# Layer 0 of a four-layer cross-attention stack by heads: raw exponentials transposed, their sums from matmuls of ones, the division after the value product, and a schedule one tick shorter

## The chip, the cores and the metric

The kernel runs on one core of a Trainium2 chip. The metric is device time in microseconds. Three timed runs of the kernel before gave 2430.0, 2432.49 and 2432.74, median 2432.49. The execution that the hardware profiler recorded took 2433.93, of which 2431.9 is the span of the trace.

## The reference, cut to what matters

All is in float32. There are B = 8 sequences of S = 256 tokens of width D = 128, and for each a context of M = 64 vectors of width 64. Layer 0, the part that changes, is attention of the tokens to the context with 16 heads of 8 channels:

```python
q = (x @ Wq.T).reshape(B, L, H, D).transpose(0, 2, 1, 3)      # H=16 heads of 8
k = (ctx @ Wk.T).reshape(...) + pos ;  v = (ctx @ Wv.T).reshape(...)
attn = softmax(q @ k.T * 8 ** -0.5)                            # over 64 context vectors
memory_output = (attn @ v).reshape(B, L, D) @ Wo.T
gate = sigmoid(silu([x, mean(ctx)] @ gate_w1.T + gate_b1) @ gate_w2.T + gate_b2)
enhanced = layernorm(x + gate * memory_output)
x = where(entropy(softmax(x @ ent_w.T)) > 1, enhanced, x)      # per sequence
```

Layer 1 is one more cross attention with one head, layer 2 is six blocks of self attention over 256 tokens with 16 heads of 64, cross attention to the context with 16 heads, and a feed-forward part; layer 3 is a last attention with a layer norm.

## The kernel before

A sequence is two tiles of 128 tokens. The tiles of layer 0 are worked through one by one, n = 2b + qt, n = 0 to 15, and all work of the kernel is laid out by hand on a grid of ticks: `at(tick, phase, step)` puts a step at a place, and at the end all steps are issued by tick, then by phase, with an ordering edge between each instruction and the one before it on its engine. So TensorE (PE), VectorE (DVE), ScalarE (ACT) and GpSimd (POOL) each work in the order of the plan, strictly. DMAs are not held by these edges.

In layer 0 a tile passes four ticks (`plan_weights_64`, L314). In tick n, phase 1, `scores` makes 16 small matmuls (L328) into a PSUM tile of 128 x 1024: 32 tokens by 16 heads by 64 keys in each group of partitions. In phase 2, `lower` copies it to SBUF on ACT (L357), takes the maximum of each head on DVE (L359) and subtracts it on POOL (L360). In phase 8 ACT takes the exponentials (L366). In tick n+1, phase 2.4, `divide` sums each head's 64 exponentials (L370), takes the reciprocal of 16 sums (L371) on DVE and multiplies on POOL (L372). In tick n+2, phase 2.5, `turn` transposes 32 x 32 blocks on DVE (L380). In tick n+3, phase 3.0, `sums` adds eight matmuls (L388) of the weights with VW, in which the value and output weights are already folded together, and `add` (L687) applies the gate and adds the residual. The same function serves the cross attention of layer 2, with a mask, in which nothing changes.

The fold is made once at the start: `spread_outputs` (POOL, L523), `turn_values` (PE L530, ACT L533), `fold_l0` (PE L545, ACT L552); for each sequence `values_of` multiplies it with the context (PE L303) and copies it (ACT L309). In ticks 1 and 2 the start also holds `gate_hidden` (L501 on ACT and L502 on DVE in turns), the mask conversions (DVE L624), `gates` (PE L508) and `logits` (PE L447).

After attention, `moments`, `normal`, `scaled` and `mix` make the layer norm of a sequence, with two transposes on PE in two different ticks (L713, L721) and small operations on POOL (L265 to L696). Layer 1 of the sequence starts two ticks later (`plan_l1`): transposes (L749), weights (L757, L761, L766, L772), another transpose (L780), values (L789, L794). Self attention of sequence b starts with its scores (L898) at tick T0 + 4b, with T0 = 17; its statistics come six ticks ahead, its normalisation (L832) five, its projections (L861, L880) four to one.

All PSUM tiles come from one pool of four slots of two banks each, taken in the order of the plan: the fifth tile waits until the first has been read. The functions that the diff touches follow.

Of the kernel before, what the change touches and what calls it, by code (L numbers as in the profile page):

```python
# [27 lines left out]
def tile_xattn_stack(ctx: ExitStack, tc: tile.TileContext, io, out: bass.AP):  # L28
# [22 lines left out]
    def tp_tile():  # L51
        return one_bank("tp")
# [137 lines left out]
        nc.vector.tensor_copy(hmask8[rows], hmask[rows, 8 * r : 8 * r + 8])  # L190


    W = {}

    def load_sa(l):
# [118 lines left out]
    def plan_weights_64(tick, qt, qT, keys, values, mask, take):  # L314

        tl = {}

        def scores():  # L320
            sc = two_banks("sc").rearrange("p (q x) -> p q x", q=4)
            if mask is None:
                for i in range(4):
                    for a in range(4):
                        q = (i + 2 * (a // 2)) % 4
                        rows = slice(64 * (a // 2), 64 * (a // 2) + 64)
                        qb = 4 * qt + q
                        nc.tensor.matmul(  # L328
                            sc[32 * a : 32 * a + 32, q, :],
                            lhsT=qT()[rows, qb * 32 : (qb + 1) * 32],  # L330
                            rhs=keys()[rows, 4 * (a % 2) : 4 * (a % 2) + 4, :].rearrange(
                                "p h k -> p (h k)"
                            ),
                            start=True, stop=True,
                        )
                tl["sc"] = sc.rearrange("p q x -> p (q x)")
                return
            for q in range(4):
                qb = 4 * qt + q
                for a in range(4):  # L340
                    nc.tensor.matmul(  # L341
                        sc[32 * a : 32 * a + 32, q, :],
                        lhsT=qT()[:, qb * 32 : (qb + 1) * 32],
                        rhs=keys()[:, a].rearrange("p h k -> p (h k)"),
                        start=True, stop=False,
                    )
                for a in range(4):
                    nc.tensor.matmul(
                        sc[32 * a : 32 * a + 32, q, :], lhsT=ones0, rhs=mask,
                        start=False, stop=True,  # L350
                    )
            tl["sc"] = sc.rearrange("p q x -> p (q x)")

        def lower():
            sc = tl.pop("sc")
            e = big("e", shape=(P, 16, M))
            nc.scalar.copy(e.rearrange("p h k -> p (h k)"), sc)  # L357
            m = sm([P, 16], "m16")
            nc.vector.tensor_reduce(m, sc.rearrange("p (h k) -> p h k", k=M), AX.X, ALU.max)  # L359
            nc.gpsimd.tensor_tensor(  # L360
                e, e, m.unsqueeze(2).to_broadcast([P, 16, M]), ALU.subtract
            )
            tl["e"] = e

        def exps():
            nc.scalar.activation(tl["e"], tl["e"], AF.Exp)  # L366

        def divide():
            r = sm([P, 16], "r16")
            nc.vector.tensor_reduce(r, tl["e"], AX.X, ALU.add)  # L370
            nc.vector.reciprocal(r, r)  # L371
            nc.gpsimd.tensor_tensor(  # L372
                tl["e"], tl["e"], r.unsqueeze(2).to_broadcast([P, 16, M]), ALU.mult
            )

        def turn():
            e = tl.pop("e").rearrange("p (q h) (k x) -> p (h k) q x", q=4, x=32)
            eT = big("k" if mask is None else "o", shape=(P, 8, 4, 32))
            for i in range(2):
                nc.vector.transpose(eT[:, 4 * i : 4 * i + 4], e[:, 4 * i : 4 * i + 4])  # L380
            tl["eT"] = eT

        def sums():
            ps = mm_tile()
            eT, vw = tl.pop("eT"), values()
            for s in range(8):
                g, r, k = s // 4, s // 2 % 2, s % 2
                nc.tensor.matmul(  # L388
                    ps[:, :D], lhsT=eT[:, s].rearrange("p q x -> p (q x)"),
                    rhs=vw[:, r, k, g, :], start=(s == 0), stop=(s == 7),  # L390
                )
            take(ps)

        at(tick, 1, scores)
        at(tick, 2, lower)
        at(tick, 8, exps)
        at(tick + 1, 2.4, divide)
        at(tick + 2, 2.5, turn)
        at(tick + 3, 3.0, sums)


    S0 = {}
# [91 lines left out]
            S0["h"].append(ps)  # L494

    def gate_hidden():
        S0["hs"] = [big("k"), big("k")]
        for b in range(B):
            h = S0["hs"][b // 4][:64, (b % 4) * S : (b % 4 + 1) * S]
            ps = S0["h"][b // 4][:64, (b % 4) * S : (b % 4 + 1) * S]  # L500
            nc.scalar.activation(h, ps, AF.Sigmoid, bias=cg[:, b : b + 1])  # L501
            nc.vector.scalar_tensor_tensor(h, ps, cg[:, b : b + 1], h, ALU.add, ALU.mult)  # L502
# [15 lines left out]
        nc.vector.tensor_copy(flag, ps[:, :B])  # L518
        nc.vector.tensor_scalar(nflag, flag, -1.0, 1.0, ALU.mult, ALU.add)

    def spread_outputs():
        S0["wobd"] = place("first", H * D).rearrange("p (h d) -> p h d", h=H)
        nc.gpsimd.tensor_tensor(  # L523
            S0["wobd"], w0o.unsqueeze(1).to_broadcast([P, H, D]),
            hmask.unsqueeze(2).to_broadcast([P, H, D]), ALU.mult,
        )

    def turn_values():
        tps = tp_tile()
        nc.tensor.transpose(tps[:, :DM], w0v, ident[:DM, :DM])  # L530
        wv2 = S0["wv2"] = place("second", P)
        for r in range(2):
            nc.scalar.copy(wv2[:, r * DM : (r + 1) * DM], tps[:, :DM])  # L533

    def fold_l0():


        wobd, wv2 = S0["wobd"], S0["wv2"]
        S0["WVO"] = sb([P, HC, D], "WVO", 1, heap)
        wvo = S0["WVO"].rearrange("p (g a) d -> p a g d", g=2)  # L540
        for half in range(2):
            ps = two_banks("mm")
            for i in range(2):
                a = 2 * half + i
                nc.tensor.matmul(  # L545
                    ps[:, i * 512 : (i + 1) * 512], lhsT=wv2,
                    rhs=wobd[:, 4 * a : 4 * a + 4].rearrange("p h d -> p (h d)"),
                    start=True, stop=True,
                )
            for r in range(2):  # L550
                rows = slice(r * DM, (r + 1) * DM)
                nc.scalar.copy(  # L552
                    wvo[rows, 2 * half : 2 * half + 2],
                    ps[rows].rearrange("p (a g r d) -> p a g r d", a=2, g=2, r=2)[:, :, :, r, :],
                )

    def fold_l1():

# [77 lines left out]
    def plan_start():  # L636
        at(-4, 0, lambda: turn_x(0))
        at(-4, 1, keys_l0)
        at(-4, 2, pool_context)
        at(-1, 0, spread_outputs)  # L640
        for c in range(1, 4):
            at(0, 3.1 + 0.1 * c, lambda c=c: turn_x(c))
        at(0, 3.6, gate_context)
        at(1, 3.0, gate_inputs)
        at(1, 3.1, gate_hidden)
        at(1, 3.2, turn_values)
        for i in range(4):
            at(1, 8.5, lambda i=i: mask(i))
        at(1, 8.6, store_masks)
        at(2, 3.1, fold_l0)  # L650
        at(2, 3.4, gates)
        at(2, 3.6, logits)
        at(3, 4, entropy)
        at(3, 4.1, fold_l1)
        at(4, 4, flags)
        at(4, 4.1, fold_l1_keys)
        at(5, 4, fold_l1_values)
        at(6, 4, fold_l1_outputs)
        at(7, 4, values_l1)
        at(16, 6, mask_keys)  # L660

    def plan_l0(b, T):
        st = {}
# [14 lines left out]
            )  # L678

        def make_values():  # L680
            st["VW"] = values_of(b, S0["WVO"])

        def add(qt, ps):
            if qt == 0:
# [13 lines left out]
        def normal():  # L698
            y = st["y"]
            for j in range(QT):  # L700
                nc.scalar.activation(
                    y[:, j, :], y[:, j, :], AF.Identity, scale=st["rstd"][:, j : j + 1],
                    bias=st["nm"][:, j : j + 1],
                )
            st["kept"] = sb([P, QT, D], "tb", 3)
            nc.scalar.mul(st["kept"], tt(b), nflag[:, b : b + 1])

# [20 lines left out]

        at(T - 2, 3.3, queries)
        at(T - 2, 7, spread_keys)  # L730
        at(T + 2, 3.2, make_values)
        for qt in range(QT):
            plan_weights_64(
                T + qt, qt, lambda: st["q"], lambda: st["k"], lambda: st["VW"], None,
                lambda ps, qt=qt: add(qt, ps),
            )
        at(T + 4, 6, moments)
        at(T + 5, 2.95, normal)
        at(T + 5, 4.8, scaled)
        at(T + 6, 4.7, mix)  # L740

    def plan_l1(b, T):

# [33 lines left out]
        def turn():  # L777
            nc.vector.reciprocal(st["r"], st["r"])
            tps = tp_tile()
            nc.tensor.transpose(tps[:, :P], st.pop("e"), ident)  # L780
            st["eT"] = sb([P, P], "o0")
            nc.scalar.copy(st["eT"], tps[:, :P])

        def values():
# [439 lines left out]
    plan_start()  # L1224
    for b in range(B):
        plan_l0(b, 2 * b)
        plan_l1(b, 2 * b + 7)
    T0 = 2 * B + 1
    T_end = {}
    for l in range(NL):  # L1230
        T_ca = T0 + 4 * B
# [108 lines left out]
```

## Time and profile before

| what | value |
|---|---|
| median of three runs | 2432.49 us |
| the profiled execution | 2433.93 us |
| its span | 2431.9 us, mean granted TensorE clock 0.986 |
| scores of layer 0, first start of ticks 0, 1, 2, 3 | 9.83, 16.60, 22.24, 47.75 us |
| ticks 8 to 13 | 83.43, 89.99, 95.19, 102.62, 107.78, 117.64 us |
| ticks 14, 15 | 129.57, 138.05 us |
| first self-attention scores (tick 17) | 151.90 us |
| L388, one tick | 16 records of 275 ns, about 1.98 us from start to next start |
| L303, one sequence | 32 records, 1.02 us from start to next start |
| L359, L370 | 1222 and 1209 ns |
| L360, L372 | 1902 and 1902 ns |

The page counts each float32 matmul as two records, and the records overlap, so the mean duration of one says less than the distance from one group's start to the next. Start times are from the start of the span. A row of groups gives line, engine, operation, the tiles written and read, shapes and count, then busy us and mean ns, then the idle time of the engine just before and what ended it. The granted clock is TensorE's, 1.00 for full speed.

### The profile page before, as it was taken

How to read it: one execution, taken by the hardware profiler on the slowest of the kernel's cores; microseconds unless marked ns; L12 is line 12 of the kernel's file. 1: busy time of each engine (PE TensorE's matmuls, PEld its weight loads, DVE VectorE, ACT ScalarE, POOL GpSimd, SP SyncE). 2: the span in 40 equal slices, each digit the busy share in tenths (PEclk: the TensorE clock that was granted, in tenths of full speed). 3: DMA queues.
4: the chain of work that ended last, by engine and by line, in shares of the span. 5: the costliest groups of instructions: out<-in, count | busy, mean ns of one | idle time of the engine just before them, and what ended most of it. 6: DMA issues, size and time to landing. Idle time of an engine off the chain costs nothing.

```text
span 2431.9 us, 99981 instructions
## 1 busy us (share of the span) xinstructions
PE 2349.5 (97%) x42411; PEld 1741.0 (72%) x42411; DVE 1836.6 (76%) x5988; ACT 1719.9 (71%) x4528; POOL 1450.3 (60%) x2483
## 2 busy tenths in 40 slices
PE   8999999999999999999999999999999999999997
PEld 4667777677777777777777777777777777777675
DVE  4778887667888667888667888667888667888674
ACT  4567777667777667777667778567778657778662
POOL 3754556755556755556765556765555765555774
PEclk9999999999999999999999999999999999999998
DMA  6000022001022001012000012000013000011000
GB/s 178 2 2 20 20 72 65 2 3 30 20 64 73 3 3 30 20 55 73 12 2 26 23 52 77 12 2 18 25 43 85 21 2 18 25 28 39 2 4 16
DMA packets 102833, 76.87 MB, mean 32 GB/s; under 512 B 8114, under 2 KB 96882, under 8 KB 102387
## 3 DMA queue, kind: packets, MB, share of 16 engines
q1 hardware_dynamic: 101794, 70.16, 10.4%
q8 instruction: 333, 5.46, 1.0%
q14 instruction: 114, 0.93, 0.1%
q10 hardware_dynamic: 592, 0.33, 0.1%
HBM read 62.07 MB, written 8.39 MB: 29 GB/s over the span
## 4 chain that ended last, share of the span: by engine, by line
PE 79%; DVE 7%; ACT 7%; POOL 5%; issue 2%; DMA 0%; SPq 0%; POOLq 0%; DVEq 0%; ACTq 0%
PE mm L861 14%; PE sc L898 14%; PE mm L953 13%; PE mm L971 7%; PE mm L880 7%; PE mm L388 5%; PE sc L341 4%; PE mm L1137 3%; PE mm L1120 3%; DVE m L359 2%; ACT e L357 2%; POOL e L360 2%; PE mm L303 1%; PE tp L841 1%; PE mm L1079 1%
## 5 line engine op out<-in xcount | busy, mean ns | idle before, releaser
L927 POOL TENSOR_SCALAR e<-e,rs 128x256 f32<-128x256 f32 x1536 | 703.1, 478 | 674.9 <-DVE rs L925 665.6
L917 ACT ACTIVATE e<-e,mn 128x256 f32<-128x256 f32 x1536 | 758.2, 495 | 133.7 <-DVE mn L912 129.4
L912 DVE CUSTOM_DVE_ANT_0 e<-sc,nm 128x256 f32<-128x256 f32 x1536 | 542.5, 419 | 108.8 <-PE sc L898 106.2
L937 DVE STREAM_TRANSPOSE eTc<-e 128x512 f32<-128x512 f32 x768 | 517.3, 695 | 62.9 <-POOL e L927 61.6
L898 PE MATMUL sc<-k,q 64*32 64x256 f32 x12288 | 378.3, 380 | 1.9 <-ACT q L867 0.9
L953 PE MATMUL mm<-eTc,v 32*64 32x256 f32 x12288 | 363.7, 378 | 5.7 <-ACT AT L1054 3.3
L953 PEld LDWEIGHTS mm<-eTc,v 32*64 32x64 f32 x12288 | 276.8, 131 | 89.1 <-issue 22.4
L360 POOL TENSOR_TENSOR e<-e,m 128x1024 f32<-128x1024 f32 x112 | 213.1, 1903 | 208.4 <-DVE m L359 208.4
L359 DVE TENSOR_REDUCE m<-sc 128x16 f32<-128x1024 f32 x112 | 136.8, 1221 | 263.8 <-ACT e L357 263.8
L898 PEld LDWEIGHTS sc<-k,q 64*32 64x32 f32 x12288 | 220.9, 106 | 123.3 <-issue 49.6
L917 ACT ACTIVATION_READ_ACCUMULATOR e<-e,mn 128x1 f32 x1536 | 287.2, 187 | 0.0
L341 PE MATMUL sc<-q,tT 128*32 128x256 f32 x3072 | 218.6, 384 | 2.3 <-DVE t L1104 2.3
L372 POOL TENSOR_TENSOR e<-e,r 128x1024 f32<-128x1024 f32 x112 | 213.0, 1902 | 1.2 <-DVE r L371 1.2
L388 PE MATMUL mm<-v,o 128*128 128x128 f32 x1536 | 199.3, 285 | 0.2 <-ACT v L309 0.2
L388 PEld LDWEIGHTS mm<-v,o 128*128 128x128 f32 x1536 | 185.6, 198 | 15.9 <-issue 8.1
L861 PE MATMUL mm<-tT,w_sk 128*128 128x256 f32 x768 | 189.1, 389 | 0.0
L971 PEld LDWEIGHTS mm<-w_sow,o 128*128 128x128 f32 x1536 | 175.1, 192 | 16.2 <-issue 12.3
L880 PE MATMUL mm<-w_sv,tT 128*32 128x256 f32 x3072 | 185.7, 382 | 0.0
L286 ACT COPY v<-mm 128x1024 f32<-128x1024 f32 x96 | 97.2, 1013 | 124.1 <-PE mm L880 123.5
L971 PE MATMUL mm<-w_sow,o 128*128 128x128 f32 x1536 | 183.4, 278 | 0.7 <-ACT WVO L1052 0.7
L861 PE MATMUL mm<-tT,w_sq 128*128 128x256 f32 x768 | 173.6, 379 | 0.0
L861 PEld LDWEIGHTS mm<-tT,w_sk 128*128 128x128 f32 x768 | 138.1, 190 | 44.1 <-issue 29.2
(212 smaller groups left out, 3551.0 us busy)
## 6 DMA issues: line engine op xcount, KB each, us to landing
nm<-mask_d SPq DMA_DIRECT2D x192, 128.0 KB
wd<-o SPq DMA_DIRECT2D x48, 128.0 KB
w_sk<-in_L_sa_kv_dram SPq DMA_DIRECT2D x6, 512.0 KB
w_sv<-in_L_sa_kv_dram SPq DMA_DIRECT2D x24, 128.0 KB
w_sq<-in_L_sa_q_dram SPq DMA_DIRECT2D x6, 512.0 KB
w_sow<-in_L_sa_ow_dram SPq DMA_DIRECT2D x6, 512.0 KB
w_ckv<-in_L_ca_kv_dram SPq DMA_DIRECT2D x12, 256.0 KB
w_cq<-in_L_ca_q_dram SPq DMA_DIRECT2D x6, 512.0 KB
```

Of the source, the lines that this page charges most:

```text
L341: nc.tensor.matmul(sc[32 * a : 32 * a + 32, q, :], lhsT=qT()[:, qb * 32 : (qb + 1) * 32], rhs=keys()[:, a].rearrange("p h k -> p (h k)"), ...
L360: nc.gpsimd.tensor_tensor(e, e, m.unsqueeze(2).to_broadcast([P, 16, M]), ALU.subtract)
L388: nc.tensor.matmul(ps[:, :D], lhsT=eT[:, s].rearrange("p q x -> p (q x)"), rhs=vw[:, r, k, g, :], start=(s == 0), stop=(s == 7),)
L861: nc.tensor.matmul(ps[:, i * S : (i + 1) * S], lhsT=w[:, c * P : (c + 1) * P], rhs=st["tT"], start=True, stop=True,)
L880: nc.tensor.matmul(ps[32 * a : 32 * a + 32, i, :], lhsT=st["tT"][:, kb * 32 : (kb + 1) * 32], rhs=sv[:, a].rearrange("p g x -> p (g x)"), ...
L898: nc.tensor.matmul(sc[32 * a : 32 * a + 32, r, j, :], lhsT=st["q"][g][rows, a, qb * 32 : (qb + 1) * 32], rhs=st["k"][g][rows, a, :], start ...
L912: nc.vector.tensor_tensor_reduce(e[:, i, :], sc4[:, i, :], st["nm"][:, 2 * jj + i % 2, :], -1.0, 3.0 * BIG, ALU.add, ALU.min, mn[:, i : i ...
L917: nc.scalar.activation(e[:, i, :], e[:, i, :], AF.Exp, scale=-1.0, bias=mn[:, i : i + 1], accum_out=rs[:, i : i + 1],)
L927: nc.gpsimd.tensor_scalar(e[:, i, :], e[:, i, :], rs[:, i : i + 1], 1.0, ALU.mult, ALU.mult)
L937: nc.vector.transpose(eT[:, r, :, 2 * jj : 2 * jj + 2, :], e[:, 2 * r : 2 * r + 2, :].rearrange("p j (k x) -> p k j x", x=32),)
L953: nc.tensor.matmul(ops[a // 2][r * HD : (r + 1) * HD, a % 2, :S], lhsT=st["v"][kb // 4][rows, kb % 4, (2 * g + r) * HD : (2 * g + r + 1) * ...
L971: nc.tensor.matmul(st["ps"][:, j * D : (j + 1) * D], lhsT=st["oT"][c // 4][:, c % 4, j * P : (j + 1) * P], rhs=sow[:, c, :], start=(c == 0 ...
```

## The change

In layer 0 (where there is no mask) the exponentials are no longer divided before they are transposed. `turn` takes them raw. `sums_by_head` then makes two products on PE, into two banks of one PSUM tile: with `cones`, a constant of ones in four blocks of 32 rows by 8 columns, it gets each head's sum, repeated over the head's 8 channels; with the head's values, spread into four blocks in the same way, it gets the unnormalised outputs, channels on the partitions. DVE takes the reciprocal of the 128 x 128 sums and multiplies the outputs by it on the way out of PSUM, and a new step, `outputs`, makes one matmul with Wo, whose rows are permuted once at the start (`turn_outputs`). The fold of values and outputs goes, and with it `spread_outputs`, `turn_values` and `fold_l0`.

The plan moves too: exponentials of tile n come in tick n+1 at phase 2.05, behind the copy of tile n+1; transposes in n+1 at 2.5; the sums in n+2 at 3.0; the outputs in n+2 at 4.6. The values are made in the sequence's second tick. The layer norm's steps, layer 1 and all that follows, `mask_keys` included, start one tick earlier (T0 = 16). The rest of the diff moves buffers: `gate_hidden` uses other ones, two tiles of layer 1 and of the new step share one, `keep` is split from `normal`.

```diff
+    cmask = const.tile([P, 4], F32, tag="cmask", name="cmask")
+    nc.gpsimd.memset(cmask, 1.0)
...
+    cones = const.tile([P, 4, 8], F32, tag="cones", name="cones")
+    nc.gpsimd.tensor_copy(cones, cmask.unsqueeze(2).to_broadcast([P, 4, 8]))
...
+        def sums_by_head():
+
+            ps = two_banks("mm").rearrange("p (i x) -> p i x", i=2)
+            eT, vw = tl.pop("eT"), values()
+            for i in range(2):
+                for k in range(2):
+                    for j in range(4):
+                        nc.tensor.matmul(
+                            ps[32 * j : 32 * j + 32, i, :P],
+                            lhsT=cones.rearrange("p a f -> p (a f)") if i == 0
+                            else vw[:, 4 * k + j, :],
+                            rhs=eT[:, 2 * j + k].rearrange("p q x -> p (q x)"),
+                            start=(k == 0), stop=(k == 1),
+                        )
+            r = sb([P, P], "r0", 2)
+            nc.vector.reciprocal(r, ps[:, 0, :P])
+            tl["oT"] = sb([P, P], "o0", 3)
+            nc.vector.tensor_tensor(tl["oT"], ps[:, 1, :P], r, ALU.mult)
+
+        def outputs():
+            ps = mm_tile()
+            nc.tensor.matmul(
+                ps[:, :D], lhsT=tl.pop("oT"), rhs=S0["wo"], start=True, stop=True
+            )
+            take(ps)
...
-        at(tick, 8, exps)
-        at(tick + 1, 2.4, divide)
-        at(tick + 2, 2.5, turn)
-        at(tick + 3, 3.0, sums)
+        if mask is None:
+            at(tick + 1, 2.05, exps)
+            at(tick + 1, 2.5, turn)
+            at(tick + 2, 3.0, sums_by_head)
+            at(tick + 2, 4.6, outputs)
+        else:
+            at(tick, 8, exps)
+            at(tick + 1, 2.4, divide)
+            at(tick + 2, 2.5, turn)
+            at(tick + 3, 3.0, sums)
...
-        S0["hs"] = [big("k"), big("k")]
+        S0["hs"] = [big("o"), big("o")]
...
-    def spread_outputs():
-    def turn_values():
-    def fold_l0():
+    def turn_outputs():
+
+        perm = place("first", P)
+        nc.gpsimd.tensor_copy(
+            perm.rearrange("p (j a f) -> p j a f", j=4, a=4),
+            ident.rearrange("p (a j f) -> p j a f", j=4, a=4),
+        )
+        ps = mm_tile()
+        nc.tensor.matmul(ps[:, :D], lhsT=perm, rhs=w0o, start=True, stop=True)
+        S0["wo"] = place("first", D)
+        nc.vector.tensor_copy(S0["wo"], ps[:, :D])
...
-            st["VW"] = values_of(b, S0["WVO"])
+            ps = mm_tile()[:, : 2 * 32].rearrange("p (k x) -> p k x", k=2)
+            for k in range(2):
+                for a in range(4):
+                    nc.tensor.matmul(
+                        ps[32 * a : 32 * a + 32, k, :],
+                        lhsT=ctx2[:DM, b, 32 * k : 32 * k + 32],
+                        rhs=w0v[:, 32 * a : 32 * a + 32], start=True, stop=True,
+                    )
+            st["VW"] = big("v")[:, :256].rearrange("p (s x) -> p s x", x=32)
+            nc.vector.tensor_tensor(
+                st["VW"].rearrange("p s (a f) -> p s a f", a=4),
+                ps.rearrange("p k (j f) -> p (k j) f", j=4).unsqueeze(2).to_broadcast(
+                    [P, 8, 4, 8]
+                ),
+                cmask.unsqueeze(1).unsqueeze(3).to_broadcast([P, 8, 4, 8]), ALU.mult,
+            )
...
-        at(T + 2, 3.2, make_values)
+        at(T + 1, 3.2, make_values)
...
-        at(T + 4, 6, moments)
-        at(T + 5, 2.95, normal)
-        at(T + 5, 4.8, scaled)
-        at(T + 6, 4.7, mix)
+        at(T + 3, 6, moments)
+        at(T + 4, 2.95, normal)
+        at(T + 4, 4.9, keep)
+        at(T + 4, 4.8, scaled)
+        at(T + 5, 4.7, mix)
...
-        plan_l1(b, 2 * b + 7)
-    T0 = 2 * B + 1
+        plan_l1(b, 2 * b + 6)
+    T0 = 2 * B
```

## The prediction

> **What bounds the kernel now.** I read the page's busy times first, then the stretches between landmarks of the trace, the chain of waits inside layer 0, the costliest groups, and TensorE's order of time with its clock.
>
> ```profile
> PE 2349.5 (97%) x42411; PEld 1741.0 (72%) x42411; DVE 1836.6 (76%) x5988; ACT 1719.9 (71%) x4528; POOL 1450.3 (60%) x2483
> ```
> TensorE is busy nearly throughout, so removed matmuls are worth time wherever it stays busy. The landmarks are the score matmuls (L328) of tick 3 at 47.75 us, of tick 13 at 117.64, and the first self-attention scores (L898, tick 17) at 151.90. Columns after the stretch: its length, then busy us of PE, PEld, DVE, ACT and POOL (instructions), then the granted clock.
>
> ```profile
> 0.00:47.75 47.75, 37.29 (x219) 18.45 (x219) 18.28 (x41) 21.03 (x31) 17.36 (x21) 0.89 0.75 206
> 47.75:117.64 69.89, 63.62 (x753) 43.87 (x752) 55.49 (x108) 40.63 (x69) 49.94 (x45) 0.98 0.08 15
> 117.64:151.90 34.26, 32.94 (x360) 23.89 (x361) 21.09 (x49) 21.17 (x37) 19.20 (x20) 0.95 0.00 1
> 151.90:2431.90 2280.00, 2215.67 (x41081) 1654.77 (x41080) 1741.74 (x5792) 1637.08 (x4392) 1363.85 (x2397) 0.99 0.10 29
> ```
> Ticks 3 to 12, layer 0 almost alone, take 69.9 us with PE busy 63.6; undisturbed, two ticks take 12.6 us (94.61 to 107.20 below). Start us, duration, what:
>
> ```profile
> 94.61 1.91 POOL e L360
> ...
> 96.54 1.06 ACT e L366
> 97.60 0.91 ACT e L357
> ...
> 98.54 1.23 DVE m L359
> 99.76 1.14 DVE r L370
> ...
> 101.17 1.16 DVE k L380 x2
> ...
> 107.20 1.91 POOL e L360
> ```
> Every engine has a part in this chain, but PE has hardly a gap beside it: it never waits for a result made in its own tick. That is what the change gives up.
>
> **The change, part by part.** What goes, in a tick: the sum L370 (1.21 us DVE), the reciprocal of 16 (0.25), POOL's product L372 (1.90), eight matmuls L388 (1.98 PE); every second tick L303 (1.02 PE) and L309 (1.01 ACT). Once: fold_l0's 5.4 us of PE (L545), L552's copies (2.3 ACT), spread_outputs (3.6 POOL).
>
> What comes, in a tick: sixteen matmuls of 32 columns (32 records), one outputs matmul (0.3 us, as a pair of transposes L713), a reciprocal of 128x128, a product. Nearest to the sixteen is L303, also 32 records, four column groups at once: 1.0 us; the other end, L388's 124 ns a record without overlap, is 4 us. I take 1.0; they have about 3.4 us from the scores' end to the reciprocal, so only the dear end would show, by 0.6 a tick. make_values: eight small matmuls, 0.35 us at L303's rate, and a DVE product near L724's 0.48 (between L687's 0.31 and twice L724); I take 0.4 from start to next start. Its ACT copy is gone.
>
> The reciprocal matters most:
>
> ```profile
> L687 DVE SCALAR_TENSOR_TENSOR y<-mm,gate,t 128x128 f32<-128x128 f32 x16 | 5.0, 313 | 0.0
> L371 DVE RECIPROCAL r<-r 128x16 f32<-128x16 f32 x16 | 4.0, 253 | 0.6
> L925 DVE RECIPROCAL rs<-rs 128x4 f32<-128x4 f32 x20 | 3.1, 154 | 1.9 <-ACT e L917 1.8
> ```
> From 4 to 16 elements it grows by 99 ns, 8.25 ns each; 112 more give 253+924 = 1.18 us. An ordinary pass of 128 takes 0.31 (L687). I take 1.1 net of overlap. So DVE trades 1.46 us for 1.5 and wins nothing.
>
> Per tick PE falls by about 1.98-1.3 = 0.7, plus 0.35 from make_values: 17 us over 16 ticks, and 5.7 with the fold and its transpose, some 23 us in all. It would all be won if PE stayed the bound. It doesn't, because of the order. On PE, outputs of tick n-2 (phase 4.6) stands ahead of the scores of tick n+1, and waits for DVE's product, which stands behind max and turn of its tick. Behind the waiting outputs matmul are mix or scaled and the next scores; for those scores wait ACT's copy, then DVE. This is a closed loop, once a tick. With start-to-next-start times from the trace: scores to copy 1.99 (83.43 to 85.42), copy to max 1.04, max 1.15, turn 1.16, reciprocal 1.1, product 0.31, hand-over to PE 0.13 (94.54 to 94.67), outputs and the two transposes 0.6: 7.5 us. In odd ticks the scores' PSUM slot also waits for the two L794 behind the values product (0.4+0.6 instead of 0.6): 7.9. Against 6.3 now. POOL and ACT sit inside: exps after the next copy takes 1.06, beside max.
>
> Start: tick 2's scores now need the buffer that gate_hidden holds, but its end (29.2, L502's last; ACT and DVE alternate as before) stays. After it on DVE: the permuted weights' copy 0.3, values product 0.4, four mask conversions (L624, 2.6) to 32.5, max 33.7, turn 34.8, reciprocal and product 36.3, eight entropy copies 36.9; the gates' matmuls (4.9) end there too; logits 5.7 to 42.6. Tick 3 begins at about 43.0, 4.7 early: the fold was ahead of gates and logits. store_masks moves some 1 us later on SP, ahead of weights not needed for 80 us: nothing. Constants on POOL lie before 8.74, where it waited for L411: nothing. Residual and key products on POOL gain room.
>
> Ticks 3 to 11, by the loop: 7.5, 8.7 (a table load before exps, and flags), 7.5, 7.5, 8.6 (the 1.23 us of L608 hold the slot), 7.5, 7.9, 7.5, 9.2 (L832, 1.3, now between turn and reciprocal): 71.9. Tick 12, which now takes the place of 13, begins at 114.9 instead of 117.64: -2.7. Ticks 12 to 15 carry self-attention projections; 12 is PE-bound at 10.7 and 13 to 15 stay in the loop, 7.9, 7.5, 9.2: 35.3 against 34.3. Ticks 16 and 17 save 0.2. Net -1.9 so far: the tick saved is a long one's worth of work pushed together.
>
> **The clock.** The loop leaves PE 2.2 to 3.3 us a tick without matmuls (after L1's or queries' matmuls at 3.6 to 4.7 us into the tick, until 6.9). Columns as above, then start, duration, engine, line:
>
> ```profile
> 64.00:66.00 2.00, 0.88 (x8) 0.62 (x6) 1.97 (x3) 0.04 (x1) 1.45 (x5) 1.00 0.00 0
> 66.00:67.00 1.00, 0.44 (x2) 0.25 (x2) 0.97 (x3) 1.00 (x3) 1.00 (x2) 0.95 0.00 0
> 67.00:68.00 1.00, 0.89 (x9) 0.42 (x13) 1.00 (x3) 0.90 (x3) 1.00 (x1) 0.50 0.02 8
> ```
> ```profile
> 67.48 3.30 PE L328 MATMUL sc<-q,xn 64*32 64x256 f32 x32
> 89.99 1.93 PE L328 MATMUL sc<-q,xn 64*32 64x256 f32 x32
> ```
> PE idled 1.63 us, with only transposes around (64.6 to 67.4), and the clock fell to 0.50: the same scores took 3.30 instead of 1.93. The Trainium skill ("TensorE: Matmul & The Clock Gate", "HAM oscillation — how this bites in real kernels") warns only of idle gaps above about 3.4 us; by that rule my loop keeps its clock and the sum stays -1.9. By the row, 2.8 us with only transposes were enough, whereas 1.4 us before 95.19 did no harm. The row decides. As its observation window need not line up with a gap, I charge half of the twelve loop-bound ticks (3 to 11, 13 to 15) with 1.37: +8.2. Ends: none, and all twelve, +16.4.
>
> Sum: -4.7 + 2.0 + 1.0 - 0.2 + 8.2 = +6.3. The profiled execution took 2433.9 (span 2431.9 and 2.0 around it) and would become 2440; the median of the runs is 1.4 lower: **2439**.
>
> **Rivals.**
> - Loop, but full clock: 2432.5-1.9, about 2431. For it: the skill's threshold, and other gaps of 1.4 us. Against it: 64 to 70 us.
> - Faster: the reciprocal runs at an ordinary pass's rate, 0.3 instead of 1.1, which shortens each loop by 0.8 to 6.7 and the gap with it below 2 us, so the clock holds: -1.9-12x0.8, about 2421. It decides the sign from about 0.6 us downwards. Against it: 8.25 ns an element.
> - Half clock in every tick: 2432.5-1.9+16.4 = 2447. For it: all gaps exceed 1.6 us. Against: a slowed tick has shorter gaps.
> - That the rest of the kernel gains from "one tick less": against it, 151.90 to the end holds the same work with PE busy 97%.
>
> **Numbers.** Chances: mixed clock 0.52 (2434 to 2446), full clock 0.22 (2426 to 2435), quick reciprocal 0.13 (2416 to 2426), every tick slow 0.13 (2443 to 2454). A measurement can tell about 0.2%, 4.9 us. Faster, below 2427.6: 0.13 + 0.04 = 0.17. Within: 0.18 of full clock and 0.10 of mixed, 0.28. Slower: 0.42 + 0.13 = 0.55. The range 2424 to 2449 leaves out most of the quick case and a third of the slowest.
>
> **What would show it.** Tick pairs of 15 us or more in ticks 8 to 11 instead of 12.6; TensorE's outputs matmul waiting on DVE's product there; a reciprocal of about 1.2 us; score groups of 3.3 us beside ones of 1.9; tick 3's scores near 43. I am wrong if the pairs stay under 13 us, or if the time after the first self-attention scores, 2280.0, changes by over 3 us.

## The result, and the profile after

The changed kernel takes 2435.9 us (median of 12 runs, 2432.13 to 2440.17), the kernel before on the same chip 2431.5 (12 runs, 2426.21 to 2435.07). The ratio is 1.0018, interval 1.0009 to 1.0027: slower by 4.4 us. The profiled execution took 2438.97 (span 2437.3, mean granted clock 0.981) where that of before took 2433.93.

First the page's busy times, to be held against the first line shown of before:

```profile
PE 2339.4 (96%) x42564; PEld 1730.1 (71%) x42564; DVE 1833.6 (75%) x5997; ACT 1708.0 (70%) x4514; POOL 1418.0 (58%) x2471
```

TensorE has 10 us less busy time, POOL 32 and ACT 12, DVE is 3 lower: every engine works less, and the span is 5.4 us longer. So the busy shares don't tell the story; the stretches between landmarks do. The landmarks are the same score matmuls (now L343): tick 3 at 42.68 us, tick 12 (which stands where 13 stood) at 121.53, the first self-attention scores at 157.57 and the fifth at 196.03. Columns as before: length, busy us of PE, PEld, DVE, ACT, POOL, then the granted clock.

```profile
0.00:42.68 42.68, 33.93 (x231) 17.60 (x231) 18.70 (x44) 17.47 (x24) 10.83 (x23) 0.84 0.69 195
42.68:121.53 78.85, 57.71 (x786) 35.93 (x785) 49.45 (x109) 33.67 (x65) 29.53 (x34) 0.86 0.13 33
121.53:157.57 36.04, 30.76 (x435) 21.07 (x435) 21.92 (x51) 20.27 (x37) 13.61 (x17) 0.97 0.01 2
157.57:196.03 38.46, 33.91 (x588) 22.79 (x588) 30.15 (x118) 29.05 (x93) 17.84 (x40) 0.91 0.06 16
196.03:2437.30 2241.27, 2183.09 (x40529) 1632.67 (x40528) 1713.35 (x5679) 1607.52 (x4300) 1346.18 (x2357) 0.99 0.10 29
```

The last stretch of before, from its fifth self-attention scores (38.06 us behind the first), is not shown there:

```profile
189.96:2431.90 2241.94, 2182.07 (x40529) 1631.16 (x40528) 1713.95 (x5679) 1608.58 (x4300) 1346.01 (x2357) 0.99 0.11 29
```

From the fifth self-attention scores on, the same work takes the same time (2241.27 against 2241.94). All of the loss lies ahead: -5.1 to tick 3, +9.0 in ticks 3 to 11 (nine ticks, against the ten ticks 3 to 12 of before), +1.8 in 12 to 15, +0.4 up to the fifth scores. In ticks 3 to 11 PE is busy 57.7 of 78.9 us, and at a clock of 0.86 instead of 0.98. The chain of waits there shows why; here is the end of tick 9's turn of it and the whole of tick 10's (start, duration, what):

```profile
100.85 0.85 DVE r L413
...
101.93 0.41 DVE v L713
102.35 0.53 DVE t L835 x2
...
103.01 3.64 PE sc L343 x32
...
106.67 1.02 ACT e L372
...
107.72 1.22 DVE m L374
108.94 1.21 DVE k L395 x2
110.15 0.85 DVE r L413
...
111.03 0.29 DVE o L415
...
111.47 0.46 PE mm L419 x2
111.93 0.22 PE tp L753 x2
```

Scores, copy, maximum, turn, reciprocal, product, outputs, transposes, and the next scores: a tick's scores now wait for a chain that began with the previous tick's scores. The pieces follow each other with no gap over 0.2 us. In tick 9, whose scores began at 94.47, the values product (L713) and the gated sum (L835) stand in the outputs' place: the next scores waited for their PSUM slot, which L835 frees.

TensorE's own waits in ticks 3 to 11 of after (us, times, longest):

```profile
PE mm L419 <- DVE o L415: 11.1, 5, 3.5
PE mm L419 <- DVE r L819: 4.1, 2, 2.0
PE mm L419 <- DVE flag L565: 2.4, 1, 2.4
```

L415 is the product; L819 and L565 are the DVE instruction just behind it, so these 17.6 us are one kind of wait. In the same ticks of before the longest waits of TensorE were:

```profile
PE tp L841 <- DVE y L687: 1.9, 1, 1.9
PE tp L713 <- ACT y L701: 1.6, 1, 1.6
```

The granted clock of after at the start of tick 10's scores, in stretches of 1 us (the clock is the third figure from the end), and then TensorE in order of time around two ticks, with its idle time in brackets:

```profile
102.00:103.00 1.00, 0.68 (x4) 0.49 (x5) 1.00 (x6) 0.00 (x0) 0.00 (x0) 1.00 0.00 0
103.00:104.00 1.00, 0.99 (x12) 0.68 (x16) 0.96 (x5) 0.70 (x4) 0.00 (x0) 0.55 0.00 0
```

```profile
60.01 0.46 PE L419 MATMUL mm<-eTc,o 128*128 128x128 f32 x2 [2.43 <-DVE flag L565]
...
60.62 1.93 PE L343 MATMUL sc<-q,xn 64*32 64x256 f32 x32
...
102.16 0.46 PE L419 MATMUL mm<-eTc,o 128*128 128x128 f32 x2 [1.36 <-DVE o L415]
...
103.01 3.62 PE L343 MATMUL sc<-q,xn 64*32 64x256 f32 x32 [0.17 <-DVE t L835]
```

After 1.36 us of idle time tick 10's scores run at half clock nearly throughout, 3.62 us instead of 1.93; after 2.43 us tick 5's scores run at full clock. The length of the last idle time alone does not decide it. Of the nine score groups of ticks 3 to 11 five took 2.8 to 3.6 us. Last, the groups of the new operations in the first 240 us (busy us, mean ns):

```profile
L413 DVE RECIPROCAL r<-mm 128x128 f32<-128x128 f32 x16 | 14.8, 922 | 0.0
L415 DVE TENSOR_TENSOR o<-mm,r 128x128 f32<-128x128 f32 x16 | 4.7, 292 | 0.5
L713 DVE TENSOR_TENSOR v<-mm,cmask 128x256 f32<-128x256 f32 x8 | 3.3, 414 | 0.0
```

### The profile page after: what moved, and what is told of

It is laid out like the page before. It is cut to its first block, busy times and chain, and to the rows that moved or that the text cites. A ratio compares the mean times of both kernels' runs of the same rounds, so it can differ in the third digit from the quotient of the medians.

```text
span 2437.3 us, 100280 instructions
## 1 busy us (share of the span) xinstructions
PE 2339.4 (96%) x42564; PEld 1730.1 (71%) x42564; DVE 1833.6 (75%) x5997; ACT 1708.0 (70%) x4514; POOL 1418.0 (58%) x2471
## 4 chain that ended last, share of the span: by engine, by line
PE 80%; DVE 7%; ACT 7%; POOL 4%; issue 1%; DMA 0%; SPq 0%; ACTq 0%; POOLq 0%; DVEq 0%
PE mm L902 14%; PE sc L939 14%; PE mm L994 14%; PE mm L1012 7%; PE mm L921 7%; PE mm L429 5%; PE sc L356 4%; PE mm L1178 3%; PE mm L1161 3%; DVE m L374 2%; ACT e L372 2%; PE sc L343 2%; PE mm L1120 2%; PE tp L882 2%; ACT e L958 1%; PE mm L318 1%
## 5 line engine op out<-in xcount | busy, mean ns | idle before, releaser
L387 POOL TENSOR_TENSOR e<-e,r 128x1024 f32<-128x1024 f32 x96 | 182.6, 1902 | 0.5 <-DVE r L386 0.5
```

## The experiments

My theory was that the new order closes a loop through TensorE and DVE once a tick, and that with the idle time in it some score groups fall to half clock. Rivals: DVE simply has too much work (the reciprocal); the clock is the whole loss; moving the later steps one tick earlier loses time; the start gains less than the fold's removal should. Each kernel is the changed one with the edit shown; "before" is the kernel before, timed with it on the same chip. The landmark I follow is the start of the fifth self-attention scores: 189.96 us before, 196.03 after.

### The loop

**The reciprocal replaced by a copy.** The outputs of layer 0 are then not divided by the sums.

```diff
-            nc.vector.reciprocal(r, ps[:, 0, :P])
+            nc.vector.tensor_copy(r, ps[:, 0, :P])
```

> The reciprocal of 128x128 (0.92 us) becomes a copy of the same shape, so the outputs of layer 0 are not divided by the sums. Loop theory (the scores of the next tick wait behind outputs, which wait for the product): each loop-bound tick is shorter by 0.92-0.3 = 0.6 us, 12 such ticks, 7 us, and a little clock: about 2428. Rival, TensorE and VectorE simply have too much work in these ticks, and the reciprocal is beside it: VectorE loses 16 x 0.6 of busy time, but TensorE's order doesn't move: within 2 us of 2435.9.

Measured: 2428.87 us (before 2432.61), ratio 0.9989, 0.9981 to 0.9997. The row of the copy:

```profile
L413 DVE COPY r<-mm 128x128 f32<-128x128 f32 x16 | 4.1, 255 | 0.0
```

It takes 667 ns less than the reciprocal. Tick 3 begins where it did (42.34), tick 12 at 109.37 instead of 121.53, the fifth scores at 184.27. Two thirds of a microsecond in each of nine ticks are 6.0 us of these 12.2. Another 4.6 are clock, perhaps since shorter loops leave shorter gaps: one score group of ticks 3 to 11 ran at half clock instead of five, with 1.7 us above 1.93 in all instead of 6.3. The remaining 1.6, of which 0.3 is the earlier start, I have not followed. The run shows that DVE's chain sets the ticks, but not whether the amount of DVE's work does it or its place in the loop. The next two tell that apart, because they take nothing from DVE.

**The sums' reciprocal and product ahead of the turn.**

```diff
-            at(tick + 2, 3.0, sums_by_head)
+            at(tick + 2, 2.4, sums_by_head)
```

> Only the phase of sums_by_head changes, 3.0 to 2.4: on VectorE reciprocal and product now come before the transposes of the same tick. Loop theory: 1.2 us leave the path in even ticks, in odd ticks the layer 1 steps behind the transposes hold the PSUM slot, so about 0 to 0.5 there: 7 ticks x 1.2, and a smaller gap for the clock (-3): about 2425. Rival, VectorE's total work bounds the tick: nothing leaves VectorE, 2436.

Measured: 2423.80 us (before 2432.61), ratio 0.9970, 0.9958 to 0.9982; first self-attention scores at 143.46 instead of 157.57. Ticks 3 to 11 took 67.8 us instead of 78.9. Three of their score groups still ran at half clock, with 3.8 us above 1.93 in all instead of 6.3, so about 8.5 of the 11.0 us come from the order and not from the clock.

**The same, and the turn behind the outputs.**

```diff
-            at(tick + 1, 2.5, turn)
-            at(tick + 2, 3.0, sums_by_head)
+            at(tick + 1, 4.55, turn)
+            at(tick + 2, 2.4, sums_by_head)
```

> As sums_before_turn, and the transposes go to phase 4.55, behind layer 1's steps and ahead of the outputs' gated sum. Loop theory: 1.2 us leave the path in all twelve loop-bound ticks (14 us) and the gap without matmuls falls to about 1 to 2 us, so most of the clock loss (8 us) goes too: 2416 (2412 to 2422), faster than both kernels. Rival, VectorE's total work bounds: 2436.

Measured: 2421.56 us (before 2432.61), ratio 0.9961, 0.9949 to 0.9973; the fifth scores at 177.82. DVE in order of time in this kernel:

```profile
80.81 1.23 DVE L374 TENSOR_REDUCE m<-sc 128x16 f32<-128x1024 f32 x1 [0.46 <-ACT e L372]
81.95 0.95 DVE L413 RECIPROCAL r<-mm 128x128 f32<-128x128 f32 x1
82.93 0.29 DVE L415 TENSOR_TENSOR o<-mm,r 128x128 f32<-128x128 f32 x1
...
83.21 1.28 DVE L395 STREAM_TRANSPOSE k<-e 128x512 f32<-128x512 f32 x2
```

The turn, which nothing in this tick needs, now runs while TensorE goes on. TensorE in the same kernel:

```profile
83.97 1.93 PE L343 MATMUL sc<-q,xn 64*32 64x256 f32 x32
...
89.65 0.46 PE L419 MATMUL mm<-eTc,o 128*128 128x128 f32 x2 [0.18 <-DVE o L415]
...
90.49 1.93 PE L343 MATMUL sc<-q,xn 64*32 64x256 f32 x32 [0.17 <-DVE t L835]
```

The outputs of tick 9 wait 0.18 us here instead of 1.36 (those of ticks 8 and 10 wait 0.84 and 0.87 instead of 2.03), two ticks take 12.8 us (83.97 to 96.75), and every score group from tick 3 to tick 11 runs at full clock. Ticks 3 to 11 took 62.6 us, 16.3 less than in the changed kernel. Of these the score groups' clock is 6.3; the other 10.0 are 1.1 us a tick, close to the 1.2 of the turn that left the path. The same DVE instructions with nearly the same durations, in another order, with TensorE's order in these ticks unchanged, are worth 12 us (sums_before_turn: 0.9970 against 1.0018) to 14 us (0.9961). That refutes the rival that DVE has too much work, and shows the loop.

**One more wait out of the way.** In that kernel tick 11 still took 8.54 us. I put it down to the normalisation for self attention on DVE (1.2 us, between the product and L713 and L835, which free the next scores' PSUM slot) and moved it behind the outputs. The wait on TensorE before that move:

```profile
103.79 0.44 PE L761 MATMUL tp<-ident,tT 128*128 128x128 f32 x2 [0.91 <-DVE v L713]
```

```diff
-        ahead(b, (T - 6, 8.3), (T - 5, 2.6), (T - 5, 7.2), norm_g, norm_b, st, False)
+        ahead(b, (T - 6, 8.3), (T - 5, 4.56 if b < 2 else 2.6), (T - 5, 7.2), norm_g, norm_b, st, False)
```

> sums_before_late_turn, and the two normalisations of self attention that fall into layer 0 (ticks 11 and 15, 1.2 us of VectorE each) go behind the transposes, from phase 2.6 to 4.56. Loop theory: they stand ahead of the layer 1 sums that hold the PSUM slot of the next scores, so 1.2 us leave the path twice: fifth self-attention tick at about 175.5 instead of 177.8, and 2419 instead of 2421.6. Rival, those ticks are bound elsewhere (ticks with projections): no change.

Measured: 2425.32 us (before 2432.65), ratio 0.9977, 0.9969 to 0.9985; the fifth scores at 179.79, a miss. Tick 11 took 8.58 us. TensorE in this kernel:

```profile
106.41 0.59 PE L882 MATMUL tp<-ident,xn 128*128 128x128 f32 x2 [1.72 <-DVE xn L873]
106.92 3.32 PE L343 MATMUL sc<-q,xn 64*32 64x256 f32 x32
```

The normalised tile is transposed on TensorE in the same tick (L882), ahead of the next scores, so the wait went from L761 to L882. I had looked at who was late, and not at who else reads what I moved. Besides, the score groups of ticks 6 and 9 ran at half clock in this trace (3.09 and 3.12 us), which they did not in the kernel above, though the edit touches ticks 11 and 15 alone. Ahead of tick 9's scores both traces have the same idle times, 0.71 and then 0.84 us. So idle times as short as these don't decide the clock by themselves; what did is not shown.

### The clock

**TensorE filled.** Two more rounds of sixteen matmuls each per tick, all with ones (the expectation counts them as four of eight), into columns of the PSUM tile that nobody reads.

```diff
+            for _ in range(2):
+                for i in range(2):
+                    for k in range(2):
+                        for j in range(4):
+                            nc.tensor.matmul(
+                                ps[32 * j : 32 * j + 32, i, 256 : 256 + P],
+                                lhsT=cones.rearrange("p a f -> p (a f)"),
+                                rhs=eT[:, 2 * j + k].rearrange("p q x -> p (q x)"),
+                                start=(k == 0), stop=(k == 1),
+                            )
```

> The sums' matmuls with ones are made four more times into unused columns (64 further records of about 32 ns, 2 us of TensorE a tick) in the stretch where TensorE waits for the product. Clock theory: the gap without matmuls falls below 1.5 us, all score groups of ticks 3 to 11 and 13 to 15 take 1.93 us, and the time falls by 7 x 1.2 = 8 us against the changed kernel, to about 2428, although 32 us of TensorE work is added. Rival, the clock costs nothing because the loop has slack or because TensorE's work is what bounds: 2436 or up to 30 us more.

Measured: 2436.27 us (before 2432.61), ratio 1.0020, 1.0010 to 1.0030. TensorE in this kernel (lines are ten higher than in the changed one):

```profile
89.86 0.46 PE L429 MATMUL mm<-eTc,o 128*128 128x128 f32 x2 [1.22 <-DVE r L829]
...
90.47 1.93 PE L343 MATMUL sc<-q,xn 64*32 64x256 f32 x32
...
98.17 1.93 PE L343 MATMUL sc<-q,xn 64*32 64x256 f32 x32 [0.17 <-DVE t L845]
```

All score groups of ticks 3 to 11 take 1.93 us. This is the loop at full clock: 7.7 us for an odd tick (90.47 to 98.17), 7.4 for the even one after it, and 72.45 us for ticks 3 to 11 (42.41 to 114.86) instead of 78.85. So in the profiled execution of after the clock cost at least 6.4 us there; somewhat more, since in tick 7 the filler was itself in the way (9.66 us, against 9.35 in after with a half-clock group). But in ticks 12 to 15, which are full of projections, the filler is work on TensorE: they took 40.2 us instead of 36.0, and the fifth scores began at 194.51, only 1.5 earlier. The median is where the rival had it, and did not fall.

**Filled to tick 11 only.**

```diff
-            for _ in range(2):
+            for _ in range(2 if tick + 2 < 12 else 0):
```

> The four more rounds of matmuls with ones only in ticks 2 to 11, where layer 0 has TensorE almost alone, and none in the ticks with self-attention projections. Clock theory: in the trace the scores of tick 12 start near 115 instead of 121.5, and nothing is added after that: the changed kernel's 2435.9 falls by 6 to 7, to about 2429.5. Rival, the earlier start is given back later (the whole run with the filler everywhere came out at 2436.3): within 1.5 us of 2435.9.

Measured: 2434.57 us (before 2432.95), ratio 1.0009, 1.0001 to 1.0018; tick 12 at 115.61, 5.9 earlier than in the changed kernel, but the fifth scores only 2.4 earlier, at 193.65. The median fits the rival (within 1.5 us of 2435.9) better than the 2429.5 expected. Two of its score groups after that, on TensorE:

```profile
115.61 3.57 PE L343 MATMUL sc<-q,xn 64*32 64x256 f32 x32
...
142.52 3.35 PE L343 MATMUL sc<-q,xn 64*32 64x256 f32 x32
```

From tick 12 to the first self-attention scores (154.06) it is 38.45 us, 2.4 more than in the changed kernel; 2.1 of these are the two half-clock groups of ticks 12 and 15 (in the changed kernel tick 12's took 2.91 and tick 15's 1.93). Another 1.1 us go between the first and the fifth self-attention scores.

**Filled there too, but thinly:** two rounds of sixteen to tick 11, none in 12, one in 13 to 15.

```diff
-            for _ in range(2):
+            for _ in range({12: 0, 13: 1, 14: 1, 15: 1}.get(tick + 2, 2 if tick < 10 else 0)):
```

> Four more rounds of matmuls with ones up to tick 11, none in tick 12 (bound by TensorE), two in ticks 13 to 15, none later. In pe_filled_to_tick_11 the scores of tick 15 and the self-attention scores of tick 16 fell on a slow clock (3.35 and 3.14 us) and gave back 2.6 of the 5.9 us gained by tick 12. Clock theory: with the later gaps closed too, the fifth self-attention tick's scores start near 191 instead of 193.7 (196.0 in the changed kernel), and the median is about 2431.5. Rival, what was gained is given back by waits that have nothing to do with the clock: 193.5 or more.

Measured: the fifth scores at 191.23 as expected, 4.8 us earlier than in the changed kernel, but 2435.34 us (before 2432.65), ratio 1.0014, 1.0005 to 1.0022: the median, expected at 2431.5, did not follow the landmark.

**The changed kernel and the one filled to tick 11 once more, on one chip,** since the two ratios above came from two chips.

> The changed kernel itself, beside filled_again on one chip, since medians of different chips could not settle what the clock costs in an ordinary run. Clock theory: 2436 to 2437, 2 to 6 us above filled_again. Rival, the profiled execution was a rare one: no difference from filled_again beyond 1 us.

> pe_filled_to_tick_11 again, for the pair with changed_again. Clock theory: 2431 to 2434.5; rival: the same as changed_again within 1 us.

Measured: 2436.58 us, ratio 1.0015, 1.0008 to 1.0022, for the changed kernel; 2434.69, ratio 1.0009, 0.9999 to 1.0019, filled (before 2433.47). The fifth scores began at 195.79 and 192.23. The two medians are 1.9 us apart, just short of the 2 us that the clock theory asked for and beyond the 1 us of its rival, with intervals that overlap. In the filled one two score groups (ticks 5 and 6) ran at half clock, and one (tick 6, 3.03 and 3.00 us) in each of the two filled kernels before it, so the filler does not always hold the clock.

In the traces the filler is worth 1.5 to 4.8 us at the landmark. The medians gain less than that, but not in the clock's runs alone: the copy gained 11.8 us at the landmark and by its ratio 7, the late turn 18.2 and 14. Each landmark is from one execution, and the rest of the kernel behind it varies by some 3 us from trace to trace (last section). That the clock in layer 0 costs something in each traced execution of the changed kernel is shown (its score groups in ticks 3 to 11 exceed 1.93 us by 6.3 and, in the second trace, by 6.7 together); how much of it an ordinary run pays is not settled.

### The tick, and the start

**The later steps one tick later again.** Moments, normal, keep, scaled, mix, layer 1, T0 and mask_keys go back to where they were before.

```diff
-        at(T + 3, 6, moments)
-        at(T + 4, 2.95, normal)
+        at(T + 4, 6, moments)
+        at(T + 5, 2.95, normal)
...
-        plan_l1(b, 2 * b + 6)
-    T0 = 2 * B
+        plan_l1(b, 2 * b + 7)
+    T0 = 2 * B + 1
```

> The tick given up comes back: moments, normal, keep, scaled, mix, layer 1, mask_keys and all later layers start one tick later, as before; sums_by_head and outputs stay where the change put them. Loop theory: one more loop-bound tick of layer 0 alone (8 to 9 us), of which the ticks with projections give back 3 to 4, since one tile less is worked through beside them: about 2441. Rival, starting the later layers a tick early is what costs (more work pushed together on each engine): 2433 or less.

Measured: 2437.04 us (before 2432.95), ratio 1.0017, 1.0010 to 1.0023, a miss: I had expected that it would cost time. Tick 12 begins earlier (119.08), since no projections have come to tick 11, then the ticks with projections give it all back: the first self-attention scores begin at 161.89, four microseconds later than in the changed kernel, and the fifth at 195.81 against 196.03. The tick taken out of the plan is worth nothing; its work moves.

**The later steps back in the kernel with the late turn.**

> sums_before_late_turn with the tick given back. With the loop short (6.3 us a tick), the tick is worth less: one more tick of 6.4 us, of which the ticks with projections give back about 4: 2.5 us above sums_before_late_turn's 2421.6, about 2424. If the early start of later layers costs: below 2421.

Measured: 2423.51 us (before 2432.95), ratio 0.9958, 0.9944 to 0.9973; the fifth scores at 182.85. Its traced execution started 4 us late for a reason that is not the edit's (tick 3 at 46.62, with the gates' matmuls taking 6.98 us instead of 4.20, at a granted clock of 0.50); less that, the landmark would be within 1.1 us of the 177.82 of the kernel with the late turn. The ratio agrees with that kernel's. So here too the tick is worth nothing that can be measured, and the order on DVE is worth the same with it and without it.

**The fold's matmuls put back into the start.** Four matmuls of 512 columns and four copies on ACT, with a result that nothing uses.

```diff
+    def fold_again():
+        wvo = sb([P, HC, D], "WVO", 1, heap)
+        flat = wvo.rearrange("p c d -> p (c d)")
+        for half in range(2):
+            ps = two_banks("mm")
+            for i in range(2):
+                nc.tensor.matmul(
+                    ps[:, i * 512 : (i + 1) * 512], lhsT=S0["wo"],
+                    rhs=xT[:, (2 * half + i) * 512 : (2 * half + i + 1) * 512],
+                    start=True, stop=True,
+                )
+            for r in range(2):
+                nc.scalar.copy(
+                    flat[r * 64 : r * 64 + 64, half * 512 : half * 512 + 512],
+                    ps[r * 64 : r * 64 + 64, r * 512 : r * 512 + 512],
+                )
...
+        at(2, 3.1, fold_again)
```

> Four matmuls of 512 columns and four ACT copies of 64x512, the size of the old fold, are put back ahead of gates in tick 2 (on other data, and their result is not used). If the fold's place ahead of gates and logits is what the start lost in the kernel before: tick 3's scores start 3.5 to 5 us later (46 to 48 instead of 42.7), and the time is 2440. Rival, VectorE's mask conversions and the entropy copies bound the start: 42.7 and 2436 stay.

Measured: 2440.97 us (before 2432.95), ratio 1.0036, 1.0023 to 1.0049. TensorE in the start of this kernel, of the changed kernel, and of the kernel before:

```profile
25.02 1.93 PE L343 MATMUL sc<-q,xn 64*32 64x256 f32 x32 [2.16 <-DVE o L549]
...
29.47 3.70 PE L586 MATMUL mm<-eTc 128*128 128x512 f32 x8
...
33.53 4.19 PE L555 MATMUL mm<-L_w2T,o 64*128 64x1 f32 x32
```

```profile
25.41 3.64 PE L343 MATMUL sc<-q,xn 64*32 64x256 f32 x32 [2.16 <-DVE o L549]
28.98 1.08 PE L405 MATMUL mm<-k,cones 128*32 128x128 f32 x16
...
30.85 0.96 PE L688 MATMUL mm<-eTc,eTc 128*128 128x256 f32 x2
31.74 4.20 PE L555 MATMUL mm<-L_w2T,o 64*128 64x1 f32 x32
```

```profile
28.97 5.40 PE L545 MATMUL mm<-eTc,eTc 128*128 128x512 f32 x8 [4.80 <-ACT eTc L533]
34.30 2.41 PE L303 MATMUL mm<-WVO,ctx 64*32 64x256 f32 x32
36.63 0.70 PE L667 MATMUL mm<-eTc,eTc 128*128 128x256 f32 x2
37.26 4.89 PE L508 MATMUL mm<-L_w2T,k 64*128 64x1 f32 x32
```

The fold's matmuls (L586) take 3.5 us of TensorE, but tick 3 begins only 1.8 later (44.47). I had expected 46 to 48 us, a miss. The two starts do not compare well, though: tick 2's scores, ahead of the fold, ran at full clock here and at half clock in the changed kernel, and so did the sums and the queries behind them. In sums_before_turn tick 2's scores began at 25.00 at full clock, too; tick 3 came at 41.69 there, 2.8 us before that of the kernel with the fold's matmuls. So they are worth 1.8 to 2.8 of the 5.1 us by which tick 3 begins earlier.

The traces of before and after account for the whole. In both TensorE has hardly a gap from 28.97 (28.98) to tick 3: it is busy for 18.68 of 18.79 us before, and for all of 13.70 after. The fold and L303 take 7.7 us of it in before (28.97 to 36.63), in part at half clock; in their place after has 1.9 us of sums (28.98 to 30.85). That is 5.8 us, of which queries, gates, logits and the new outputs take back 0.7. The median is 4.4 us above the changed kernel's by the ratios, although the landmark moved by 1.8 only (197.83); with four runs, I leave that open.

## Why the prediction was right, step by step

**The bound.** Right: 2439 forecast, 2435.9 measured; the profiled execution 2440 forecast and 2438.97 measured. The landmarks agree as well: the forecast's terms put tick 12 at 121.1 and the first self-attention scores at 158.4, with the clock's 8.2 us spread evenly over its twelve ticks; they came at 121.53 and 157.57. What carried it is the step "This is a closed loop, once a tick", shown by the two runs that change DVE's order alone. Counted in advance the change removes 23 us of TensorE; the page shows 10 less, since the score groups at half clock are longer (6.3 us more of that than in before). It came out slower because TensorE stopped being the bound in the stretch where the work was removed.

**The start.** Tick 3 forecast at 43.0, measured at 42.68. The reason, "the fold was ahead of gates and logits", fits the two traces, and the fold's matmuls put back show a part of it (1.8 to 2.8 us). The exact size is in part luck: the gates ended at 35.9 us, not 36.9, and the logits took 6.4 us, not 5.7, at half clock.

**The loop.** Forecast 7.5 and 7.9 us at full clock; TensorE filled showed 7.4 and 7.7. Ticks 3 to 11 were forecast at 71.9 and took 72.45 there; eight of the nine lie within 0.3 us of their forecast, and tick 7, where the filler was in the way, 1.1 above it. The pair of ticks in after, 86.43 to 103.01, is 16.6 us with half-clock groups in it, above the 15 that I had named.

**The reciprocal.** Mis-sized: 1.18 us forecast, 922 ns measured, so it grows by (922-253)/112 = 6.0 ns an element, not 8.25. Sixteen elements were too few to extrapolate from. In the loop that is 0.2 us too much, and half of it was hidden by maximum and turn, which took 0.1 more than I had put: 7.4 us instead of 7.5. The sums' two groups took 1.0 us as forecast (44.54 to 45.55), the values product 0.41.

**Ticks 12 to 15, and the two behind them.** Forecast 35.3 for ticks 12 to 15 without the clock; measured 36.04, of which 0.98 is tick 12's half-clock group, so 35.1 without it. The two ticks with the first self-attention scores were to save 0.2 and took 18.74 us (157.57 to 176.31) instead of 17.52 (151.90 to 169.42): the first score group ran at half clock, 3.62 us instead of 1.96. By the fifth group 0.8 of these 1.2 us had come back.

**The clock.** "I charge half of the twelve loop-bound ticks": for the traced executions this was right in the sum (9 x 0.69 = 6.2 forecast for ticks 3 to 11; the score groups there exceed 1.93 us by 6.3 together, and the filled kernel is 6.4 shorter). The half itself was a guess in the middle between none and all, and that it was hit is luck. Ticks 13 to 15, which I had charged too, lost nothing; tick 12, which I had not, lost 0.98. Whether an ordinary run pays as much is open. In two of the filled kernels more than half of what was won by tick 12 was lost again by the fifth scores (6.7 to 1.5 us, and 5.9 to 2.4). In the third most of it stayed (6.0 to 4.8), and in the pair on one chip all of it did (3.3 to 3.6), but the medians of that pair are only about 2 us apart. The forecast with 2 to 4 in place of 8.2 would have been 2433 to 2435, 1 to 3 us below the measured 2435.9, where 2439 is 3 above it: the median can't tell the two apart.

Where I set the trace against the Trainium skill ("TensorE: Matmul & The Clock Gate", "HAM oscillation — how this bites in real kernels"), the trace was the better guide: of the waits ahead of the half-clock groups only one, 3.51 us, reached the length that the page names; the others were 1.4 to 2.1 us. But my own reading, "1.4 us before 95.19 did no harm", was no rule either. It counted transposes with the idle time, which was 0.45 us there; and in the changed kernel 1.36 us of idle time before tick 10 did harm, while 2.43 before tick 5 and 2.03 before tick 11 did none. The same page's next section ("A second HAM failure mode: psum-queue depth-cycling") speaks of frequent short idle times that make the clock swing. Tick 10 would fit, since its 1.36 us came with 0.78 us of idle time less than 3 us earlier; tick 11 does not, with 0.62 and then 2.03 us within 2.5 us of each other and full clock behind them. What share of busy time is needed, and over what stretch, no run here measures.

**The rest.** "151.90 to the end holds the same work": 2280.0 before, 2279.7 after. The rival that one tick less brings something falls by later_steps_back and by late_turn_later_steps_back. The rival of a loop at full clock (2431) falls for the traced execution; the rival of a quick reciprocal would have been right in its mechanism: the copy is 0.67 us quicker, four of the five half-clock groups went, and the kernel came out just ahead of before (0.9989, 0.9981 to 0.9997), by some 3 us and not that rival's 11.5.

**A version that beats both kernels** is the changed kernel with the sums' reciprocal and product ahead of the turn, and the turn behind the outputs: 0.9961 of before (0.9949 to 0.9973), with nothing but two phase numbers changed.

## What to carry to other kernels

When a step that was taken from work several iterations old is brought closer, walk along the in-order queues from its result back to itself: if the way crosses two engines and ends within one iteration, the sum of its durations is the new iteration time wherever it is longer than each engine's own work, whatever the busy shares say, and removed work on the engines beside it is worth nothing. Then look on the slow engine for work in the loop that nothing in this iteration needs, and put it behind the result that another engine waits for; ask who else reads what is moved. A gain at a landmark in the middle of a kernel is a gain only if the landmarks behind it move as well.

## What was not expected of the hardware

- The changed kernel's second profiled execution repeats the first within 0.4 us at the landmarks up to the fifth self-attention scores (42.32 and 42.68 for tick 3, 195.79 and 196.03), though ticks between them start up to 2.4 us apart (tick 9 at 91.99 and 94.40), and then takes 3.5 us less for the same instructions. Its last stretch:

```profile
195.79:2433.60 2237.81, 2178.73 (x40529) 1628.22 (x40528) 1713.25 (x5679) 1608.19 (x4300) 1347.99 (x2357) 0.99 0.10 29
```

  The first execution has 2241.27 us there, so the difference between these two lies behind layer 0. In all fourteen traces of this case that stretch, the same work in each, took 2237.8 to 2244.6 us; that 2241.27 and 2241.94 in the result's comparison agree to 0.7 us is therefore in part chance, and the sign of being wrong that I had named, a change of over 3 us behind the first self-attention scores, was set no wider than this spread.
- Over the 12 runs of the changed kernel, time and mean granted clock have a correlation of -0.86, about -1.1 us for each 0.001 of clock. A change of 0.2% has to be read against that.
- A reciprocal of 128 x 128 from PSUM takes 922 ns where a copy takes 255 and a product 292.
- A busy TensorE is not always at full clock. In late_turn_later_steps_back the granted clock was 0.50 from 30 to 40 us, though TensorE was busy for all of these 10 us, most of them with the gates' matmuls of one column (L555). What these matmuls have to do with it, no run here shows.
